# Score and softmax vectors written to HBM from their columns in natural order, without turns on TensorE; second layer's second pass moved into the projection

## The chip, the cores and the metric

The kernel runs on one core of one Trainium2 chip. The metric is device microseconds (us) of one execution. TensorE does the matrix products and writes them to its output memory, PSUM; VectorE and ScalarE work element by element; the sync engine's queue issues transfers between the on-chip memory and HBM, the memory outside the core. A transfer *lands* when it counts as complete, so that what waits for it may go on. The *granted clock* is the mean share of its full clock that TensorE was given in a run. Most executions agree within 0.3%. The kernel before was timed again in each session and took 3140 us in the first and 3148 to 3152 us in the later ones; ratios are always taken within a session.

## The reference, cut to what matters

Two graph attention layers over 32 graphs of 512 nodes, after a normalization and a ReLU; float32 throughout, with the residual x added at the end.

```python
def gat_layer(x, mask, W, a_src, a_dst, bias, concat):
    xl = (x @ W).reshape(B, N, H, F)
    asrc = einsum('bnhf,hf->bnh', xl, a_src)
    adst = einsum('bnhf,hf->bnh', xl, a_dst)
    e = leaky_relu(asrc[:, :, None, :] + adst[:, None, :, :], 0.2)
    e = where(mask[..., None], e, -1e9)
    attn = softmax(e, axis=1)
    out = einsum('bsdh,bshf->bdhf', attn, xl)
    ...
# layer 1: 4 heads of 256 features; layer 2: one head of 512
```

The scores asrc and adst come out of the projection as columns: node t*128+p sits on partition p, column t. The softmax also needs a vector of all 512 nodes laid along the free dimension of every partition. That takes a change of layout, from a column to a row spread over 128 partitions. It happens 8 times a batch: twice for the scores of layer 1 (two heads together), once for those of layer 2, and five times for the softmax result r (four heads and one head). In all there are 96 + 160 = 256 of these spreads.

## The kernel before

The layout change goes through HBM. TensorE turns (transposes) the columns, VectorE copies the turned rows out of PSUM, one transfer writes them as 8 (or 4) rows of 512 bytes, and another reads them back into all partitions. (In this code the names of the tiles are left out, and cuts are marked by dots.)

```python
def spread(self, v, rows, tag, more):
    k = rows * NT
    ps = psum.tile([k, P], F32, tag="tp", bufs=2)
    nc.tensor.transpose(ps, v, identf)              # the turn
    sb = work.tile([k, P], F32, tag="spread")
    nc.vector.tensor_copy(sb, ps)
    dr = dram.tile([k, P], F32, tag=f"d{tag}{k}")
    nc.sync.dma_start(dr, sb)                       # 8 x 512 bytes
    o = work.tile([P, 2, N], F32, tag=f"o{tag}", bufs=2)
    nc.sync.dma_start(o[:, :rows]..., <dr read by all 128 partitions>)
    return o

def first(self, h):     # leaky relu of asr + ad, mask, exp, sums; gives r
    ...                 # reads the spread scores
def second(self, h):    # p = exp(max(rr0 + lo0, rr1) + lo1), masked
    ...                 # reads the spread r
```

TensorE runs in program order; the other engines' instructions are put in order when the kernel is built, by a scheduler that weighs priorities and estimated times. Each engine then works through its list in that order and waits where an input is missing.

## Time and profile before

| | before |
|---|---|
| median of three runs | 3140.7 us (3139.0 to 3141.8) |
| TensorE busy | 3036.8 us, 97% of the profiled span of 3143.5 us |
| VectorE, ScalarE busy | 79%, 57% |
| packets of the DMA engines | 121,530, of which 15,616 under 512 bytes |

The prediction shows the lines that carry its argument. One view that it did not use answers to the main view of the changed kernel: the waits of the sync queue, which issues all transfers. The columns are who waited for what, us in total, times, longest.

```profile
SPq L251 <- DMA drr<-rrr: 120.7, 100, 2.9
SPq L251 <- DMA das<-ras: 61.9, 66, 2.0
```

The queue waits for a turned vector to land before it issues the broadcast that reads it. That is 182.6 us in 166 waits, 1.1 us each; for the other 90 of the 256 it did not have to wait. The profile page of this kernel lists no landing times.

### The profile page before, as it was taken

How to read it: one execution, taken by the hardware profiler on the slowest of the kernel's cores; microseconds unless marked ns; L12 is line 12 of the kernel's file. 1: busy time of each engine (PE TensorE's matmuls, PEld its weight loads, DVE VectorE, ACT ScalarE, POOL GpSimd, SP SyncE). 2: the span in 40 equal slices, each digit the busy share in tenths (PEclk: the TensorE clock that was granted, in tenths of full speed). 3: DMA queues.
4: the chain of work that ended last, by engine and by line, in shares of the span. 5: the costliest groups of instructions: out<-in, count | busy, mean ns of one | idle time of the engine just before them, and what ended most of it. 6: DMA issues, size and time to landing. Idle time of an engine off the chain costs nothing.

```text
span 3143.5 us, 35412 instructions
## 1 busy us (share of the span) xinstructions
PE 3036.8 (97%) x11536; PEld 2027.3 (64%) x11536; DVE 2494.4 (79%) x5663; ACT 1806.2 (57%) x3873; POOL 44.0 (1%) x38
## 2 busy tenths in 40 slices
PE   5899999999999999999999999999999999999997
PEld 4566676676676666676666766666766666766654
DVE  8678887788878888877888877888878788778774
ACT  4556656556656556565566565566565565665651
POOL 0000000000000000000000000000000000000000
PEclk8999999999999999999999999999999999999998
DMA  5122232222232222222222322222322222222211
GB/s 188 44 71 84 84 101 88 81 78 91 85 98 82 86 81 87 88 93 88 71 84 85 101 90 88 74 84 85 101 88 81 78 85 90 96 84 71 65 66 62
DMA packets 121530, 269.38 MB, mean 86 GB/s; under 512 B 15616, under 2 KB 22656, under 8 KB 121344
## 3 DMA queue, kind: packets, MB, share of 16 engines
q1 hardware_dynamic: 121344, 267.12, 25.9%
q8 instruction: 90, 1.47, 0.2%
q14 instruction: 96, 0.79, 0.1%
HBM read 232.53 MB, written 34.54 MB: 85 GB/s over the span
## 4 chain that ended last, share of the span: by engine, by line
PE 78%; DVE 9%; DMA 9%; ACT 1%; SPq 1%; issue 1%; POOL 0%; DVEq 0%; ACTq 0%; POOLq 0%
PE po L414 27%; PE po L477 10%; PE pxm_0a L348 7%; PE pxm_1a L348 7%; DMA orr<-drr 4%; PE pxm_1b L348 3%; PE pxm_0b L348 3%; DVE p L310 3%; PE pxl_2a L348 3%; DVE p L318 3%; PE pxl_3a L348 3%; DMA drr<-rrr 2%; DMA x<-in_x_dram 2%; PE pxl_0a L348 2%; PE pxm_0g L348 2%; PE pxl_3b L348 2%
## 5 line engine op out<-in xcount | busy, mean ns | idle before, releaser
L414 PE MATMUL po<-p,xl 128*128 128x512 f32 x2048 | 894.0, 595 | 9.2 <-DVE p L318 9.2
L414 PEld LDWEIGHTS po<-p,xl 128*128 128x128 f32 x2048 | 388.3, 191 | 484.5 <-issue 452.1
L314 ACT ACTIVATE p<-p,lo 128x512 f32<-128x512 f32 x640 | 442.4, 719 | 254.2 <-DVE p L310 253.1
L284 DVE CUSTOM_DVE_ANT_0 l<-l,mt 128x512 f32<-128x512 f32 x640 | 415.8, 685 | 130.6 <-ACT l L281 129.5
L310 DVE SCALAR_TENSOR_TENSOR p<-orr,lo 128x512 f32<-128x512 f32 x640 | 448.4, 747 | 77.9 <-DMA orr<-drr 77.7
L281 ACT ACTIVATE l<-oas,sc 128x512 f32<-128x512 f32 x640 | 430.4, 711 | 87.8 <-DMA oas<-das 84.2
L288 ACT ACTIVATE l<-l,low 128x512 f32<-128x512 f32 x640 | 455.0, 712 | 37.8 <-DVE low L284 34.7
L477 PE MATMUL po<-xl,p 128*128 128x512 f32 x1024 | 460.6, 594 | 10.0 <-DVE p L318 10.0
L318 DVE TENSOR_TENSOR p<-p,m 128x1024 f32<-128x1024 f32 x320 | 384.2, 1218 | 0.0
L477 PEld LDWEIGHTS po<-xl,p 128*128 128x128 f32 x1024 | 187.8, 191 | 211.4 <-issue 198.8
L420 ACT ACTIVATE e<-po,b_sb 128x512 f32<-128x512 f32 x256 | 172.5, 675 | 160.5 <-PE po L414 159.1
L422 DVE SCALAR_TENSOR_TENSOR h<-po,b_sb,e 128x512 f32<-128x512 f32 x256 | 191.2, 747 | 5.4
L348 PE MATMUL pxm_0a<-w_sb,h 128*128 128x257 f32 x768 | 184.1, 382 | 0.0
L348 PE MATMUL pxm_1a<-w_sb,h 128*128 128x257 f32 x768 | 182.6, 379 | 0.0
L348 PEld LDWEIGHTS pxm_0a<-w_sb,h 128*128 128x128 f32 x768 | 144.0, 191 | 37.7 <-issue 14.0
L421 DVE TENSOR_SCALAR e<-e 128x512 f32<-128x512 f32 x256 | 107.9, 421 | 72.5 <-ACT e L420 68.5
L348 PEld LDWEIGHTS pxm_1a<-w_sb,h 128*128 128x128 f32 x768 | 143.1, 190 | 23.9
L348 PE MATMUL pxm_1b<-w_sb,hs 128*128 128x257 f32 x512 | 123.7, 384 | 5.0 <-DVE hs L331 5.0
L348 PE MATMUL pxm_0b<-w_sb,hs 128*128 128x257 f32 x512 | 121.8, 380 | 0.0
L482 DVE TENSOR_TENSOR xr<-po,xr 128x512 f32<-128x512 f32 x128 | 87.3, 682 | 43.0 <-PE po L477 42.9
L288 ACT ACTIVATION_READ_ACCUMULATOR l<-l,low 128x1 f32 x640 | 120.2, 188 | 0.0
L348 PE MATMUL pxl_0a<-w_sb,ht 128*128 128x258 f32 x372 | 99.2, 389 | 19.5 <-DVE xl L359 19.5
(137 smaller groups left out, 4048.5 us busy)
## 6 DMA issues: line engine op xcount, KB each, us to landing
orr<-drr SPq DMA_DIRECT2D x160, 512.0 KB
x<-in_x_dram SPq DMA_DIRECT2D x128, 256.0 KB
adj<-in_adj_dram SPq DMA_DIRECT2D x128, 256.0 KB
oas<-das SPq DMA_DIRECT2D x64, 512.0 KB
xr<-in_x_dram SPq DMA_DIRECT2D x128, 256.0 KB
out_dram<-xr SPq DMA_DIRECT2D x128, 256.0 KB
oas<-das SPq DMA_DIRECT2D x32, 256.0 KB
drr<-rrr SPq DMA_DIRECT2D x160, 4.0 KB
```

What stands on the lines that cost most here:

```text
L281: nc.scalar.activation(e, self.asr[i][:, j, :], AF.Prelu, bias=ad[:, d : d + 1], alpha=SLOPE)
L284: nc.vector.tensor_tensor_reduce(out=e, in0=e, in1=MASKT[self.b][:, d, :], scale=-1.0, scalar=BIG, op0=OP.add, op1=OP.min, accum_out=low[: ...
L288: nc.scalar.activation(e, e, AF.Exp, bias=low[:, d : d + 1], scale=-1.0, accum_out=tot[:, d : d + 1])
L310: nc.vector.scalar_tensor_tensor(p[:, u, :], rr[:, 0, :], lo[:, 0, j, u : u + 1], rr[:, 1, :], op0=OP.add, op1=OP.max,)
L314: nc.scalar.activation(p[:, u, :], p[:, u, :], AF.Exp, bias=lo[:, 1, j, u : u + 1])
L318: nc.vector.tensor_tensor(pp, pp, MASK[self.b][:, t : t + 2, :], op=OP.min)
L348: nc.tensor.matmul(ps, left[n][:, k, m * P : (m + 1) * P], right(w_sb[:, n - 1], k), start=(first and k == 0), stop=(k == kh - 1), skip_gr ...
L414: nc.tensor.matmul(ps, xl[:, s, h, 2 + f * P : 2 + (f + 1) * P], p[:, s, :], start=(s == 0), stop=(s == NT - 1),)
L420: nc.scalar.activation(e, ps, AF.Exp, bias=bias)
L421: nc.vector.tensor_scalar(e, e, 1.0, -1.0, op0=OP.min, op1=OP.add)
L422: nc.vector.scalar_tensor_tensor(H1[b][:, g, :], ps, bias, e, op0=OP.add, op1=OP.max)
L477: nc.tensor.matmul(ps, p[:, s, d * P : (d + 1) * P], v[:, s, 1 : DO + 1], start=(s == 0), stop=(s == NT - 1),)
```

## The change

The intent is to take the turns off TensorE, which bounds the kernel. The columns are written straight to HBM, each 4-byte element at its natural place. A softmax then no longer asks anything of TensorE, so the passes can be called in another order; the copies that empty PSUM (evacuations) become urgent, and the second pass of layer 2 moves from the start of the projection to its eighth step.

```diff
-            k = rows * NT
-            ps = psum.tile([k, P], F32, tag="tp", name=f"p{tag}{name}", bufs=2)
-            nc.tensor.transpose(ps, v, identf)
-            sb = work.tile([k, P], F32, tag="spread", name=f"r{tag}{name}")
-            nc.vector.tensor_copy(sb, ps)
-            dr = dram.tile([k, P], F32, tag=f"d{tag}{k}", name=f"d{tag}{name}")
-            nc.sync.dma_start(dr, sb)
+            dr = dram.tile([rows, NT, P], F32, tag=f"d{tag}{rows}", name=f"d{tag}{name}", bufs=3)
+            nc.sync.dma_start(dr.rearrange("r t p -> p r t"), v)
...
+            with tc.high_priority(offset=URGENT):      # around each evacuation of PSUM
...
-                        plan[2] = [lambda: late.turn(0), lambda: late.second(0)]
+                        plan[8] = [lambda: step(mt), lambda: late.second(0)]
...
-                        (3, lambda: s1.turn(0)), (3, lambda: s1.first(2)),
-                        (4, lambda: s1.second(0)),
+                        (1, lambda: s1.first(1)), (1, lambda: s1.turn(1)),
+                        (3, lambda: s1.second(0)),
...  (the rest of the new order: each turn is called right behind its first pass)
```

More of the change, by code (lines that the diff above doesn't have):

```diff
@@ L20 @@
 BIG = 2.0**100
+URGENT = 300
 def rows_of(ap, n):
@@ L205, in norm @@
                 nc.tensor.transpose(ps[:, k, :], hn[:, k * P : (k + 1) * P], identf)
-            nc.scalar.activation(HT[b][:, :, t * P : (t + 1) * P], ps, AF.Relu)
+            with tc.high_priority(offset=URGENT):
+                nc.scalar.activation(HT[b][:, :, t * P : (t + 1) * P], ps, AF.Relu)
             yield
@@ L228, in turned_masks @@
                 )
-            nc.vector.tensor_scalar_add(MASKT[b][:, d, :], ps, -BIG)
+            with tc.high_priority(offset=URGENT):
+                nc.vector.tensor_scalar_add(MASKT[b][:, d, :], ps, -BIG)
             yield
@@ L268, in rows @@
             self.asr[i] = self.spread(
-                self.sc[i][:, 0].rearrange("p h t -> p (h t)"), self.g, "as", i
+                self.sc[i][:, 0], self.g, "as", i
             )
@@ L300, in turn @@
         def turn(self, h):
-            self.rr[h] = self.spread(self.r.pop(h).rearrange("p i t -> p (i t)"), 2, "rr", h)
+            self.rr[h] = self.spread(self.r.pop(h), 2, "rr", h)
         def second(self, h):
@@ L351, in sevens @@
                 )
-            if n in (1, 5, 6):
-                nc.scalar.activation(to(*{1: (0, 0), 5: (1, 1), 6: (0, 1)}[n]), ps, AF.Copy)
-            elif n == 4:
-                nc.scalar.activation(to(1, 0), ps, AF.Copy)
-            else:
-                d = to(*{2: (0, 0), 7: (1, 1), 3: (0, 1)}[n])
-                nc.vector.tensor_add(d, ps, d)
+            with tc.high_priority(offset=URGENT):
+                if n in (1, 5, 6):
+                    nc.scalar.activation(to(*{1: (0, 0), 5: (1, 1), 6: (0, 1)}[n]), ps, AF.Copy)
+                elif n == 4:
+                    nc.scalar.activation(to(1, 0), ps, AF.Copy)
+                else:
+                    d = to(*{2: (0, 0), 7: (1, 1), 3: (0, 1)}[n])
+                    nc.vector.tensor_add(d, ps, d)
             yield
@@ L419, in gather1 @@
                 e = work.tile([P, N], F32, tag="xr", name=f"e{b}_{g}", bufs=2)
-                nc.scalar.activation(e, ps, AF.Exp, bias=bias)
-                nc.vector.tensor_scalar(e, e, 1.0, -1.0, op0=OP.min, op1=OP.add)
-                nc.vector.scalar_tensor_tensor(
-                    H1[b][:, g, :], ps, bias, e, op0=OP.add, op1=OP.max
-                )
+                with tc.high_priority(offset=URGENT):
+                    nc.scalar.activation(e, ps, AF.Exp, bias=bias)
+                    nc.vector.tensor_scalar(e, e, 1.0, -1.0, op0=OP.min, op1=OP.add)
+                    nc.vector.scalar_tensor_tensor(
+                        H1[b][:, g, :], ps, bias, e, op0=OP.add, op1=OP.max
+                    )
                 yield
@@ L531, in tile_gat @@
         s1.columns(1)
+        s1.rows(1)
+        s1.first(0)
+        s1.turn(0)
         step(nm)
-        s1.first(0)
-        s1.rows(1)
-        step(nm)
-        s1.turn(0)
         s1.first(1)
+        s1.turn(1)
         s1.second(0)
         step(nm)
-        s1.turn(1)
         s1.first(2)
+        s1.turn(2)
         s1.second(1)
+        step(nm)
+        s1.first(3)
+        s1.turn(3)
+        s1.second(2)
         step(nm)
@@ L561, in tile_gat @@
                     if late:
-                        plan[2] = [lambda: late.turn(0), lambda: late.second(0)]
+                        plan[8] = [lambda: step(mt), lambda: late.second(0)]
                     if i >= 1:
                         plan[14] = [lambda: residual_bias(i - 1)]
-                    plan[20] = [lambda: s1.columns(0)]
-                    plan[24] = [lambda: s1.rows(0), lambda: s1.first(0)]
-                    plan[28] = [lambda: s1.columns(1), lambda: s1.first(1)]
+                    plan[20] = [lambda: s1.columns(0), lambda: s1.rows(0)]
+                    plan[24] = [lambda: s1.first(0), lambda: s1.turn(0)]
+                    plan[28] = [lambda: s1.columns(1), lambda: s1.rows(1)]
                     for n, _ in enumerate(project1(i + 1), 1):
@@ L578, in tile_gat @@
                     for n, f in (
-                        (1, lambda: s1.rows(1)),
-                        (3, lambda: s1.turn(0)), (3, lambda: s1.first(2)),
-                        (4, lambda: s1.second(0)),
-                        (9, lambda: s1.turn(1)), (9, lambda: s1.first(3)),
-                        (10, lambda: s1.second(1)),
-                        (13, lambda: s1.turn(2)),
-                        (14, lambda: s1.second(2)),
-                        (16, lambda: s1.turn(3)),
+                        (1, lambda: s1.first(1)), (1, lambda: s1.turn(1)),
+                        (3, lambda: s1.second(0)),
+                        (4, lambda: s1.first(2)), (4, lambda: s1.turn(2)),
+                        (7, lambda: s1.second(1)),
+                        (9, lambda: s1.first(3)), (9, lambda: s1.turn(3)),
+                        (12, lambda: s1.second(2)),
                     ):
@@ L597, in tile_gat @@
                         15: [lambda: late.rows(0), lambda: late.first(0)],
-                        18: [lambda: late.turn(0), lambda: late.second(0)],
+                        16: [lambda: late.turn(0), lambda: late.second(0)],
                     }
@@ L612, in tile_gat @@
                 if late:
-                    plan[2] = [lambda: late.rows(0), lambda: late.first(0)]
+                    plan[0] = [lambda: late.rows(0)]
+                    plan[2] = [lambda: late.first(0), lambda: late.turn(0)]
                 if i + 2 == B:
-                    plan[6] = [lambda: late.turn(0)]
                     plan[7] = [lambda: late.second(0)]
                 if i < 0:
-                    plan[0] = [lambda: s1.turn(2), lambda: s1.first(3), lambda: s1.second(2)]
-                    plan[2] = [lambda: s1.turn(3), lambda: s1.second(3)]
+                    plan[1] = [lambda: s1.second(3)]
                 else:
```

## The prediction

> **What bounds the kernel now.** I read the page's busy shares first, then TensorE's waits, then its timeline in one steady stretch and at both ends, and last the DMA queue's own rows.
>
> ```profile
> PE 3036.8 (97%) x11536; PEld 2027.3 (64%) x11536; DVE 2494.4 (79%) x5663; ACT 1806.2 (57%) x3873; POOL 44.0 (1%) x38
> PE   5899999999999999999999999999999999999997
> DMA  5122232222232222222222322222322222222211
> ```
>
> TensorE has work in 97% of the span and misses some in the first three slices and the last. So the change can only win what TensorE idles (3143.5 - 3036.8 = 106.7 us), its own removed work, and cold-clock time; 2% is 63 us.
>
> ```profile
> PE prr L245 <- DVE r L295: 40.2, 32, 8.5
> PE pxl_0a L348 <- DVE xl L359: 19.5, 30, 1.5
> PE po L477 <- DVE p L318: 10.0, 1, 10.0
> PE pxm_1b L348 <- DVE hs L331: 5.0, 1, 5.0
> L245 PE MATMUL prr<-identf,r 128*8 128x128 f32 x160 | 43.9, 274 | 40.4 <-DVE r L295 40.2
> L245 PE MATMUL pas<-identf,sc 128*8 128x128 f32 (+1 forms) x96 | 26.1, 272 | 4.1 <-DVE sc L402 4.1
> ```
>
> Columns of the first four: who waited for whom, us in total, times, longest. The largest wait is for the turns the change removes (prr, pas). The second is the first layer's projection waiting for a VectorE addition out of PSUM, once per batch.
>
> ```profile
> 1347.79 1.03 PE L348 MATMUL pxl_0b<-w_sb,hs 128*128 128x258 f32 x4
> 1348.66 0.27 PE L245 MATMUL prr<-identf,r 128*8 128x128 f32 x1
> 1348.77 1.04 PE L348 MATMUL pxl_0g<-w_sb,ht 128*128 128x258 f32 x4
> ...
> 1361.82 1.14 PE L348 MATMUL pxl_0a<-w_sb,ht 128*128 128x258 f32 x4 [0.73 <-DVE xl L359]
> ...
> 1385.07 0.27 PE L245 MATMUL prr<-identf,r 128*8 128x128 f32 x1 [0.42 <-DVE r L295]
> ...
> 148.84 0.37 PE L245 MATMUL prr<-identf,r 128*8 128x128 f32 x1 [8.53 <-DVE r L295]
> 149.01 3.16 PE L348 MATMUL pxm_0a<-w_sb,h 128*128 128x257 f32 x8
> 152.00 1.90 PE L348 MATMUL pxm_1a<-w_sb,h 128*128 128x257 f32 x8
> ```
>
> A turn is 0.27 us long, but the next matmul starts 0.11 us after it, so 0.11 us is its price. After the 8.53 us gap eight matmuls took 3.16 us instead of 1.90.
>
> ```profile
> 26.30 1.58 SPq L149 DMA_DIRECT2D b_sb<-in_L_gnn_b_dram  x1
> 1387.12 0.28 SPq L249 DMA_DIRECT2D drr<-rrr  x1
> 1388.35 0.32 SPq L251 DMA_DIRECT2D orr<-drr  x1
> 1392.29 0.75 DVE L310 SCALAR_TENSOR_TENSOR p<-orr,lo 128x512 f32<-128x512 f32 x1 [1.06 <-DMA orr<-drr]
> 31.50:32.00 0.50, 0.50 (x4) 0.45 (x3) 0.50 (x1) 0.19 (x1) 0.00 (x0) 1.00 1.09 348
> 32.00:32.50 0.50, 0.50 (x4) 0.42 (x4) 0.50 (x3) 0.20 (x1) 0.00 (x0) 1.00 1.24 219
> DMA packets 611, 0.11 MB, mean 219 GB/s; under 512 B 510, under 2 KB 607, under 8 KB 611
> ```
>
> The first row issues the load of the bias in 4-byte elements, 128x8 of them: the same count as a new write of scores. It kept the queue 1.58 us. Today's 4 KB write lands so that the broadcast can issue 1.23 us after it, and the broadcast is usable 3.9 us later. The two windows (last two columns: DMA share and GB/s) price small packets: 31.5 to 32 had 170 packets of about 1 KB in 1.09 x 0.5 x 16 = 8.7 engine-us, 51 ns each; 32 to 32.5 had 611 packets (last row) in 9.9 engine-us, so the 510 small ones took (9.9 - 101 x 0.051) / 510 = 9 ns each.
>
> **What the Trainium skill says.** "DMA: Bandwidth & Descriptors", Rules for kernel authors: a strided last dimension becomes one descriptor per element. The bias load agrees: the small packets are there, and the issue took 1.58 us against 0.28. The same page, Two DMAs through the same engine are not ordered: a DMA that reads what another wrote has to wait for its completion; so write, landing and broadcast stay in series, as L249 and L251 are. "TensorE: Matmul & The Clock Gate", Part 1: after about 3.4 us idle the clock falls to half and needs as long to return; 3.16 against 1.90 us agrees. The same page, Part 4, has a transpose at about 275 ns in one kernel; the rows say 272 to 274, of which 0.11 us is paid in a stream.
>
> **Part by part.** One steady batch of before, from gather to gather (178.67 to 2938.98 us, 29 batches), is 95.2 us. TensorE's timeline splits it: projection one 26.7, second gather 15.0, projection two 26.0, first gather 27.6.
>
> 1. Turns removed: 256 of them, 8 a batch: 8 x 0.11 = 0.9 us a batch on the path. Their PSUM copies leave VectorE (8 x about 0.2 us), beside other work.
> 2. The waits of turns: 40.2 + 4.1 us go wholly, as TensorE no longer stands in the softmax chain; but 22.9 us of it (8.05, 6.27, 8.53) and 2.74 lie in the first 150 us, and 3.43 + 2.55 at the end. Steady share about 0.4 us a batch, with restart about 0.6.
> 3. The 0.65 us wait of pxl_0a: before, VectorE stood at L310 for a broadcast (0.71 us) and then did six second-pass operations (1356.4 to 1361.4) ahead of the addition. In the built order of after, the second layer's pass sits between the additions of the gather before it, and the additions, now urgent, follow each other. Summing VectorE's durations in that order from the last h of the gather (about 3 us into the projection), the addition ends when its matmul does, at about 10.6 us, and is needed at 14. I count 0.6 us gained.
> So the floor is 25.6 + 14.2 + 25.7 + 27.5 = 93.0 us a batch; the rest is rounding.
> 4. The new write, from column to broadcast usable: issue about 1.4, 64 packets per engine x 9 ns = 0.6 beside it, receipt about 1: 2.4 us against 1.23, then 3.9. It saves in turn the wait for TensorE's place, turn and copy: 1.4 to 5.5 us by the rows between r and the write (1384.9 to 1387.1; 1404.95 to 1410.5). The softmax is about 3 us earlier at its start, level at worst later.
> The walk through one batch of after, from projection one's start at 0, takes the built order and net durations (distance to the next start) from the timelines: softmax pass over the mask (L284) 0.61, p (L310) 0.67, p times mask (L318) 1.14, ScalarE's exponentials 0.62 to 0.71. The score columns are ready at 19, and their broadcast at 19 + 0.2 + 2.4 + 3.9 = 25.5 (before: 29.2). VectorE then does sums of h (4 x 1.14), sixteen L284, the store additions and three heads' passes without a rest. Head 0: r at 34, broadcast at 34 + 6.3 = 40, p done at 46. Head 1: r at 39, broadcast at 46, p done at 54. Head 2: r at 51, broadcast at 57, p done at 64. Head 3: r at 59, p done by about 75. The gather takes them at 65.5, 72, 79 and 86. So every head is ready 10 us or more ahead. The tightest points are two additions out of PSUM in projection two: they stand behind head 2's p, end at 59.5 and 61.8, and TensorE wants their banks at 62 and 63.8: about 2 us of slack. I allow 0.3 us a batch for what I miss: 93.3. Steady: 29 x 1.9 = 55 us.
> 5. Start: the first four softmaxes are bound by VectorE (45 of 50 us from 60 to 110), not by turns. But the order of after does less unneeded work ahead of the fourth head, ready about 98.5 instead of 105; that removes the 5.2 us wait in the gather and some of its lag: 7 us. The next batch, without a second gather, takes 66.0 us from projection to gather and needs 52: 12 us after a small allowance.
> 6. End: the last regular batch 1.6 us. In the last gather the turn's wait (3.43), the wait for hs (5.0: the second pass stood before it) and the cold clock after it (2.6) go: 11 us. In the closing chain, score column to first product took 26.1 us (3097.7 to 3123.8), of which TensorE stood 2.55 and 10.04 us; without the turns' places and copies and with slower writes about 23: 3 us.
> Sum: 55 + 19 + 1.6 + 14 = 90 us, 3051. Pieces so computed meet contention I have not seen, so I take off a tenth of the gain or less: 3057.
>
> **Rivals.** *The scattered write is slow.* 1,024 writes of 4 bytes in HBM may be acknowledged more slowly than the reads I priced. For it: no such write is in the trace. Against: the 9 ns and DMA engines busy only a quarter of the time. With 3 us more each, slack of 2 us at the tight additions is gone: 1 us a batch returns, ends lose 6: about 3095. With 8 us more the softmax bounds: slower than before.
> *VectorE takes the bound.* It is busy 75 to 77 of 95 us and nearly gapless in the last 40 us ahead of the gather; waits for broadcasts (77.7 us today) then are not absorbed by turns. Against: it loses work, and the softmax starts earlier. It would leave 1 us a batch: about 3085.
> *Only the urgent order matters:* if the removal of turns merely moves TensorE's idle time to the p tiles, the gain is 0.9 + 0.6 us a batch and little at the ends: about 3090.
> *No losses:* 93.0 a batch and better ends: about 3040.
>
> **Range and chances.** The steady floor, summed from start-to-start distances, is sure to 0.2 us; the losses on top are one-sided. 3036 to 3090 should hold it 8 times in 10. Faster by over 2% (below 3078) has 0.83, within 2% 0.15, slower 0.02.
>
> **What would show it.** Right: TensorE's busy share 99%; no wait for r or sc columns in its list; pxl_0a's wait nearly gone; batches of 93 to 93.5 us; gather one ending near 105 us; new writes issuing in 1.2 to 1.6 us, their broadcasts about 2.4 us after. Wrong: waits of po or pxm for L317 or L359 of a half us or more in each batch; more idle VectorE time before its first p operation on orr than 77.7 us with TensorE waiting behind it; a write-to-broadcast distance over 4 us; or VectorE rows of waits for adj or xr delaying additions.

## The result, and the profile after

The changed kernel took 5084.85 us (median of four runs, 5078.54 to 5091.19) against 3139.86 us before: a ratio of 1.6194 (95% interval 1.6166 to 1.6223). A version that differs from it only in the queue of the broadcasts gave right results. I had given "slower" a chance of 0.02.

The first lines are of its page: busy time, TensorE's and the DMA engines' busy tenths in 40 slices, and the packets.

```profile
PE 3357.5 (66%) x11280; PEld 2216.9 (44%) x11280; DVE 2412.2 (47%) x5407; ACT 1799.1 (35%) x3873; POOL 42.8 (1%) x38
...
PE   4766757667566675666756667666666576675766
...
DMA  4122122221222212222122221222221232212121
...
DMA packets 367542, 269.34 MB, mean 53 GB/s; under 512 B 263552, under 2 KB 268672, under 8 KB 367360
```

No engine is busy more than 66%, and the DMA engines move almost nothing: after the first slice no slice shows more than three tenths. The number of matmuls fell by exactly the 256 turns, and the small packets rose to 263,552. A kernel in which nothing is busy waits in a chain. The chain that ended last, by engine, is the next line (TensorE had 78% of this chain before, DMA 9%):

```profile
DMA 61%; DVE 17%; PE 15%; ACT 2%; issue 2%; SPq 1%; POOL 1%; DVEq 0%; POOLq 0%; ACTq 0%
```

Then TensorE's waits (columns as before). Compare them with the prediction's list, in which the largest was 40.2 us:

```profile
PE pxm_0a L347 <- ACT xl L354: 709.5, 60, 20.6
PE po L414 <- DVE p L317: 365.7, 40, 26.8
PE pxl_1g L347 <- DVE h L423: 352.6, 29, 13.5
```

The first and third are waits for a PSUM bank (one of the pieces of PSUM that TensorE writes in turn). ScalarE and VectorE would need well under 1 us to empty it, 0.37 and 0.75 us, but they stand in their own order behind other operations. What VectorE waited for among the transfers, in the same columns:

```profile
DVE p L309 <- DMA orr<-drr: 895.7, 116, 12.4
DVE stats L193 <- DMA x<-in_x_dram: 692.0, 59, 17.9
```

The first is the second pass of a softmax, which waits for its broadcast; the second is the normalization, which waits for a load of x (8.9 us in all before). What the broadcast waits for is in the waits of the sync queue:

```profile
SPq L250 <- DMA drr<-r: 1501.6, 160, 12.3
...
SPq L250 <- DMA das<-sc: 864.2, 96, 11.9
```

All 256 scattered writes are waited for, 2366 of 5083 us in all, 9.2 us each against 1.1 before. One of them can be followed: first in the queue's timeline (start, duration of the issue), then in the busy tenths of the DMA engines in 40 slices of each of the two microseconds 2218 to 2219 and 2219 to 2220, then in the window after them (window, length, busy PE, PEld, DVE, ACT, POOL, clock, DMA share, GB/s):

```profile
2217.78 0.37 SPq L248 DMA_DIRECT2D das<-sc  x1
2227.01 0.32 SPq L250 DMA_DIRECT2D oas<-das  x1
```

```profile
DMA  0000000000000000000000000001468777777777
DMA  7687677678884100000000000000000000000000
```

```profile
2220.00:2227.00 7.00, 7.00 (x36) 6.08 (x35) 4.64 (x16) 5.77 (x15) 0.00 (x0) 1.00 0.00 0
```

The issue took 0.37 us, not the 1.4 I expected. The engines handled the small packets between about 2218.7 and 2219.4, in some 0.7 us, near the 0.6 that I had priced. Then, for 7.6 us, they moved nothing, and only at 2227 did the write count as landed. So the time lies neither in the issue nor in the moving of the packets, but after it. The page's list of issues (last column: median us from issue to landing) gives the same for all of them:

```profile
drr<-r SPq DMA_DIRECT2D x160, 4.0 KB, 10.3
das<-sc SPq DMA_DIRECT2D x64, 4.0 KB, 9.7
das<-sc SPq DMA_DIRECT2D x32, 2.0 KB, 8.3
```

Half the elements (the last row has 512 of them, not 1,024) save only 1.4 us, so this is not a price per element.

The slow write also holds up what is issued behind it. Here a load of x was issued 0.5 us after a scattered write that landed at 2239.8, and VectorE, idle for 15.8 us, stood for that load until 2240.5:

```profile
2227.89 0.38 SPq L248 DMA_DIRECT2D drr<-r  x1
2228.37 0.66 SPq L178 DMA_DIRECT2D x<-in_x_dram  x1
```

By the landings in the trace, 89 transfers were issued while a scattered write was under way, and none of them landed before it. For loads of x the median to landing was 11.7 us in that case (57 of them) and 4.7 otherwise. The chain that ended last has 35% in scattered writes (drr and das), 12% in broadcasts and 15% in loads of x. So the loss has two paths, the broadcasts and the loads behind them, and both begin with the same landing.

TensorE's clock went down too, from 0.990 to 0.825: the page has 3357.5 us of busy TensorE for 11,280 matmuls, where the version of the second experiment has 2991.0 for as many at 0.990. Of every time below that has long waits of TensorE, a part is this.

### The profile page after: what moved, and what is told of

Its sections match the earlier page's. It is cut to its first block, busy times and chain, and to the rows that moved or that the text cites. A ratio compares the mean times of both kernels' runs of the same rounds, so it can differ in the third digit from the quotient of the medians.

```text
span 5083.1 us, 34627 instructions
## 1 busy us (share of the span) xinstructions
PE 3357.5 (66%) x11280; PEld 2216.9 (44%) x11280; DVE 2412.2 (47%) x5407; ACT 1799.1 (35%) x3873; POOL 42.8 (1%) x38
## 4 chain that ended last, share of the span: by engine, by line
DMA 61%; DVE 17%; PE 15%; ACT 2%; issue 2%; SPq 1%; POOL 1%; DVEq 0%; POOLq 0%; ACTq 0%
DMA drr<-r 19%; DMA das<-sc 16%; DMA x<-in_x_dram 15%; DMA orr<-drr 7%; DVE p L309 6%; DMA oas<-das 5%; DVE l L283 3%; DVE p L317 2%; PE pxl_0a L347 2%; PE pxl_1a L347 2%; PE po L478 1%; DVE h L423 1%; PE pxl_2a L347 1%; PE pxl_3a L347 1%; PE pxl_1g L347 1%
## 5 line engine op out<-in xcount | busy, mean ns | idle before, releaser
L414 PE MATMUL po<-p,xl 128*128 128x512 f32 x2048 | 977.2, 638 | 365.7 <-DVE p L317 365.7
L309 DVE SCALAR_TENSOR_TENSOR p<-orr,lo 128x512 f32<-128x512 f32 x640 | 451.3, 746 | 896.1 <-DMA orr<-drr 895.7
L347 PE MATMUL pxm_0a<-w_sb,hs 128*128 128x257 f32 x256 | 118.3, 641 | 591.9 <-ACT xl L354 585.4
L347 PE MATMUL pxm_0a<-w_sb,h 128*128 128x257 f32 x768 | 281.4, 530 | 335.8 <-DVE xl L359 211.7
L193 DVE BATCH_NORM_STATS2 stats<-x 128x6 f32<-128x512 f32 x128 | 86.4, 676 | 692.0 <-DMA x<-in_x_dram 692.0
L317 DVE TENSOR_TENSOR p<-p,m 128x1024 f32<-128x1024 f32 x320 | 385.8, 1214 | 0.6 <-ACT p L313 0.6
L347 PEld LDWEIGHTS pxm_0a<-w_sb,h 128*128 128x128 f32 x768 | 197.7, 266 | 412.0 <-DVE xl L359 223.8
L347 PEld LDWEIGHTS pxm_0a<-w_sb,hs 128*128 128x128 f32 x256 | 79.4, 325 | 622.4 <-ACT xl L354 602.4
L347 PE MATMUL pxl_1g<-w_sb,ht 128*128 128x258 f32 x124 | 62.8, 660 | 352.6 <-DVE h L423 352.6
L347 PE MATMUL pxm_1a<-w_sb,h 128*128 128x257 f32 x768 | 207.9, 418 | 5.2 <-ACT xl L354 5.2
L347 PEld LDWEIGHTS pxl_1g<-w_sb,ht 128*128 128x128 f32 x124 | 35.5, 315 | 363.1 <-DVE h L423 357.6
L347 PEld LDWEIGHTS pxm_1a<-w_sb,h 128*128 128x128 f32 x768 | 170.6, 222 | 39.7 <-ACT xl L354 5.6
## 6 DMA issues: line engine op xcount, KB each, us to landing
drr<-r SPq DMA_DIRECT2D x160, 4.0 KB, 10.3
```

Source lines behind the costliest of these rows:

```text
L193: nc.vector.bn_stats(stats[:, t, :], XT[b][t])
L309: nc.vector.scalar_tensor_tensor(p[:, u, :], rr[:, 0, :], lo[:, 0, j, u : u + 1], rr[:, 1, :], op0=OP.add, op1=OP.max,)
L317: nc.vector.tensor_tensor(pp, pp, MASK[self.b][:, t : t + 2, :], op=OP.min)
L347: nc.tensor.matmul(ps, left[n][:, k, m * P : (m + 1) * P], right(w_sb[:, n - 1], k), start=(first and k == 0), stop=(k == kh - 1), skip_gr ...
L414: nc.tensor.matmul(ps, xl[:, s, h, 2 + f * P : 2 + (f + 1) * P], p[:, s, :], start=(s == 0), stop=(s == NT - 1),)
```

## The experiments

My theory (A) was that the slow landing of scattered writes is the whole of the loss, and that the rest of the prediction's sum holds. The rivals were that the new order of work or the urgent priorities do the harm, that the blocked sync queue holds back other transfers, or that the turns' absence moves the wait elsewhere.

### Only the write, in the kernel before

```diff
-            nc.tensor.transpose(ps, v, identf) ... nc.sync.dma_start(dr, sb)
+            nc.sync.dma_start(dr.rearrange("r t p -> p r t"), v)
```

> The kernel before, with its own order of work and no urgent priorities, in which only the turn (transpose, PSUM copy, 8x512-byte write) is replaced by the write of single 4-byte elements. Theory A (the landing of that write, 8 to 12 us instead of about 1, lengthens the softmax chain by some 8 us at each of 8 writes a batch): about 3140 + 32 x 64 = 5190 us, 4700 to 5500. Rival B (the new order of work and the urgent priorities did the harm, the write is a small part): within 150 us of 3140.

It took 5177.13 us, ratio 1.6429 (1.6400 to 1.6457). The write alone, in the old order and without priorities, loses even a little more than the whole change. Theory A holds; the rival that the new order did the harm has fallen.

### Everything but the write

The changed kernel keeps its order and its priorities, but VectorE turns the vector in 32x32 blocks, and four transfers write runs of 128 bytes.

```diff
-            nc.sync.dma_start(dr.rearrange("r t p -> p r t"), v)
+            nc.vector.tensor_copy(sq[:, :k], v)          # sq: a [128, 32] pad
+            nc.vector.transpose(tq, sq)                  # 32 x 32 blocks
+            for q in range(P // 32):
+                nc.sync.dma_start(dr...[:, q * 32 : q * 32 + 32], tq[q * 32 : q * 32 + k, :])
```

> The changed kernel, whole plan and priorities kept, but each vector is turned on VectorE (one small copy, one transpose in 32x32 blocks) and written as runs of 128 bytes in four transfers, with no 4-byte elements and no turns on TensorE. Theory A (only the size of the landing was wrong in the prediction, the rest of its steps hold): 3040 to 3090 us. Rival B (the plan or the loss of turns by itself does harm): above 3200. If four transfers of 128-byte runs land as slowly as the 4-byte ones: about 5000.

It took 3059.15 us with right results, ratio 0.9703 (0.9688 to 0.9717): faster than both kernels, and 2 us from the number that I had predicted for the changed kernel. The first line is its busy time, the second TensorE's longest list entry.

```profile
PE 2991.0 (98%) x11280; PEld 2026.0 (66%) x11280; DVE 2492.0 (81%) x5923; ACT 1798.8 (59%) x3873; POOL 34.3 (1%) x38
```

```profile
PE po L428 <- DVE p L331: 23.7, 5, 15.2
```

The waits of turns are gone, and none of the waits in each batch of the changed kernel is left. The prediction's total was therefore reachable, but not with the write that it was made for.

### The priorities alone

> The kernel before with nothing but the urgent priorities around the evacuations of PSUM. Theory A (priorities are a small gain, the wait of 0.65 us at the first layer's projection mostly goes): 3100 to 3135 us. Rival B (urgent evacuations delay the softmax, part of the harm comes from there): above 3150.

The edit is the kernel before with the urgent blocks of the diff and nothing else. It took 3122.72 us, ratio 0.9904 (0.9889 to 0.9919): a gain of 1%, clear of the noise. The rival that the priorities harm has fallen.

### Turns on VectorE in the old order, without and with the priorities

> The kernel before with its own order of work and no priorities; only the turn moves from TensorE to VectorE, written as runs of 128 bytes. If the prediction's first two items hold by themselves (0.9 us a batch of turns and most of the 44 us of waits for turns): 3075 to 3110 us. If the waits only move to the p tiles, as in the rival 'Only the urgent order matters': 3105 to 3130.

It took 3097.28 us, ratio 0.9836 (0.9821 to 0.9851). Taking the turns off TensorE is worth some 52 us by itself (1.64% of 3148).

> The kernel before with its own order of work, turns on VectorE and the urgent priorities. If the two gains add up (ratios 0.9836 and 0.9904 to the kernel before): 0.974, some 3065 us, and the changed order of work is worth less than 0.5%. If the moved second pass and the new order are worth 1% or more: 3090 or more here against 3059 with them.

It took 3063.61 us, ratio 0.9733 (0.9712 to 0.9754), close to the product 0.9836 x 0.9904 = 0.9742. The two gains add up. The new order with its moved second pass, the third part of the change, is left with 0.9733 - 0.9703 = 0.3%; the two intervals overlap, so even that is not clear of the noise.

### The new order with the old turns

> The changed order of work and priorities, but the turns back on TensorE as in the kernel before. The new order puts each turn directly behind its first softmax pass, so TensorE, which works in program order, stands until r is there: some 5 turns a batch by 3 to 6 us, 3140 + 32 x 15 to 32 x 30 = 3600 to 4100 us. If the order of work does not need the turns to be off TensorE: 3060 to 3150.

One run, its state unknown, gave 3997.2 us. TensorE stands for r, as the wait shows:

```profile
PE prr L249 <- DVE r L299: 685.4, 99, 10.8
```

With the old turns the new order loses, so it could not have been tried before the turns were off TensorE.

### The broadcasts on another queue

```diff
-            nc.sync.dma_start(o[:, :rows]...)      # the broadcast only
+            nc.gpsimd.dma_start(o[:, :rows]...)
```

> The changed kernel, with only the broadcast reads issued from GpSimd's queue, so that the wait for a landing no longer holds up the loads of x, adj and the stores on the sync queue. Theory A (the chain column, scattered write, landing, broadcast, softmax is what bounds: latency): 4700 to 5100 us. Rival (the sync queue, blocked 2366 of 5083 us, holds back other transfers, and that is most of the loss): 3300 to 4200.

One run, its state unknown, gave 5218.79 us, 119 above the upper end of theory A and 1000 above what the rival allows. With the landing waited for elsewhere, the sync queue was free to issue the other transfers, and nothing was gained: that the loads are issued late is not the loss. But the run does not free the loads. Issued behind a scattered write they still landed after it (148 of 148 such transfers), loads of x took 12.2 us to land in the median, and VectorE waited longer for them than in the changed kernel (busy us, mean ns of one, idle before and what ended it):

```profile
L193 DVE BATCH_NORM_STATS2 stats<-x 128x6 f32<-128x512 f32 x128 | 88.2, 691 | 730.0 <-DMA x<-in_x_dram 730.0
```

How the loss divides between late broadcasts and late loads, no run separates.

### Only the three score vectors scattered

```diff
+            if tag == "as":  (4-byte elements, as in the changed kernel)
+            else:            (VectorE's turn, as in the second experiment)
```

> The kernel with VectorE's turns and the changed plan (3059 us), in which only the score vectors (3 of the 8 a batch) are written as single 4-byte elements. If each scattered write lies on the softmax chain with its full extra of some 8 us: 3059 + 32 x 3 x 8 = 3830, 3600 to 3900. If a softmax that starts later is hidden behind the projections as the prediction counted (10 us ahead at the gather): 3060 to 3300.

It took 3839.77 us, ratio 1.2182 (1.2161 to 1.2202). The extra over the version with all vectors turned is 3839.8 - 3059.2 = 780.6 us; by 32 batches and 3 writes that is 8.1 us for each scattered write. From the start of a write of scores to its broadcast the median is 9.8 us here and 2.3 us with all vectors turned (means 9.8 and 3.3), so the extra is 6.5 to 7.6 us. Each write costs at least that, and nothing of it was hidden behind the projections. What goes beyond it has TensorE's clock in it (0.913 against 0.990, 179 us more of busy TensorE) and VectorE's waits for loads of x (271 us against 22).

### The writes by themselves

A kernel without the GAT (wrong result) sends one transfer at a time, waits, reads 512 bytes back and goes on. In the first try the transfers were not held in program order:

> No GAT at all (wrong result on purpose): one transfer at a time on one queue, each waited for and 512 bytes of it read back before the next; six of each kind. Expected landing of the write. Theory 1 (writes that fall into the same 64 bytes are done one after the other, sixteen of them at some 0.5 us each): the natural order lands in 8 to 10 us with eight, four, two and one column alike; elements 64 or 512 bytes apart land in 2 to 3 us; pairs of 8 bytes about half, 4 to 5 us; eight elements of one partition side by side are as slow if only the shared line matters. Theory 2 (each 4-byte write costs, whatever stands beside it): the landing falls with the count, about 9, 5.5, 3.7 and 2.8 us for eight, four, two and one column, and elements far apart are as slow as neighbours, 9 us. Both: rows of 32, 128 and 512 bytes land in 1.5 to 3 us. Reads of 1,024 single elements: 2 to 3 us under theory 1, 8 under theory 2.

The scheduler laid the kinds of writes over each other, so their landings could not be told apart; it showed nothing that I use. In the second try the queue keeps its order:

> The kinds of writes of the first try again, now held in strict program order on the queue, so that the start of each 512-byte read behind a write marks the landing of that write. Theory 1 (writes into the same 64 bytes wait for each other): eight, four, two and one column in natural order land alike, 8 to 10 us; elements 64 or 512 bytes apart in 2 to 3 us; pairs in 4 to 5 us. Theory 2 (each 4-byte write costs something of its own, whatever stands beside it): about 9, 5.5, 3.7 and 2.8 us for eight, four, two and one column; elements far apart as slow as neighbours, 9 us. In both, rows of 32, 128 and 512 bytes land in 1.5 to 3 us, and 1,024 reads of 4 bytes in about 2 us (the first try had 2.3).

These are waits of the sync queue for the write to land, after its issue of about 0.4 us (who waited for what, us in total, times, longest; "eight" and "one" are 1,024 and 128 elements in natural order, "gapline" is 1,024 elements each 64 bytes apart, "rowshort" is 128 rows of 32 bytes side by side):

```profile
SPq L88 <- DMA dnateight<-src: 39.3, 4, 10.9
...
SPq L88 <- DMA dnatone<-src: 27.8, 4, 7.3
...
SPq L88 <- DMA dgapline<-src: 8.9, 4, 2.3
...
SPq L88 <- DMA drowshort<-src: 4.3, 4, 1.1
```

From the start of the write to the start of the read behind it, the means of four are:

| kind of write | writes | to landing, us |
|---|---|---|
| natural order, 8 / 4 / 2 / 1 columns | 1024 / 512 / 256 / 128 | 10.3 / 9.2 / 8.3 / 7.3 |
| the same 1,024 elements, 16 / 64 / 512 bytes apart | 1024 | 3.3 / 2.7 / 2.6 |
| 8 elements of one partition, 8 bytes apart | 1024 | 6.2 |
| pairs of 8 bytes, natural order | 512 | 3.8 |
| rows of 32 / 128 / 512 bytes | 128 / 32 / 8 | 1.5 / 1.4 / 1.3 |

Theory 2, a price for each 4-byte write, has fallen twice over. An eighth of the writes still takes 7.3 us where it had 2.8, and the same 1,024 writes land in 2.7 us once they stand apart. In this kernel the spaced elements go into a piece of HBM that was overwritten as a whole just before, and the dense ones into one that only the repetition before had written; the full kernel below, which zeroes the piece only once, at the start, gives about the same 2.7 us, so this was not the reason. Theory 1 holds in kind: what costs is how close together in HBM the written pieces stand. Its number for one column was 8 to 10 and 7.3 came out, so the count adds a little. Reads are not concerned: 1,024 reads of 4 bytes took about 2.5 us from one to the next, a small copy between them included.

A third kernel varied the step:

> One transfer at a time again. 1,024 elements of 4 bytes at steps of 4, 8, 16, 32 and 64 bytes. If what counts is how many writes share 64 bytes, each waiting some 0.5 us: 10, 6.2, 3.4, 2.9, 2.7 us from the write's start to the landing; if the shared piece is 32 bytes, 32 and 64 are equal, and if it is larger than 64 bytes nothing levels off before 64. One column (128 elements): 7.3 close together, about 2 at 64 bytes. Runs of 16 bytes (256 writes) about 3, runs of 32 bytes 1.5 us.

For steps of 4, 8, 16, 32 and 64 bytes, the means of five were 10.5, 4.5, 3.2, 2.9 and 2.7 us. The 8-byte step was nearer to the pairs than to my 6.2. Most of the price is gone at 16 bytes, and it does not level off sharply at a size of piece that I could name. One column, close together and 64 bytes apart:

```profile
SPq L88 <- DMA dcolumn<-src: 36.0, 5, 7.5
...
SPq L88 <- DMA dcolumnfar<-src: 5.3, 5, 1.1
```

The same 128 writes waited 7.2 us each, or 1.1. Runs of 16 bytes landed in 2.2 us in the mean (1.6 to 3.0), runs of 32 bytes in 1.5.

### The same writes, 64 bytes apart, in the full kernel

```diff
-            dr = dram.tile([rows, NT, P], ...)
-            nc.sync.dma_start(dr.rearrange("r t p -> p r t"), v)
+            dr = <one of three tiles [rows, NT, P, 16], zeroed at the start>
+            nc.sync.dma_start(dr[:, :, :, 0].rearrange("r t p -> p r t"), v)
```

> The changed kernel with the same 1,024 writes of 4 bytes, the same issues and the same broadcasts, but in HBM the elements stand 64 bytes apart, so that no two share 64 bytes. The broadcast still reads 4 KB in one piece, so it spreads wrong numbers (wrong result on purpose; the time does not depend on them). Theory (the loss is only that writes close together in HBM wait for each other; alone, such a write landed in 2.7 us, near the 2.4 us of the prediction): 3045 to 3100 us. Rival (many 4-byte writes are slow in the full kernel however they stand): above 4000.

It took 3217.26 us, ratio 1.0217 (1.0188 to 1.0246). Its output is wrong, which doesn't matter for the time. With the same number of 4-byte writes, 5084.9 - 3217.3 = 1868 us of the loss is gone, so the rival that such writes are slow in the full kernel however they stand has fallen. But my range ended at 3100. One wait that comes in each batch was left, and the landing was 2.9 us for r:

```profile
PE pxl_1g L359 <- DVE h L435: 97.6, 29, 5.0
```

```profile
drr<-r SPq DMA_DIRECT2D x160, 4.0 KB, 2.9
```

VectorE's timeline of one batch shows why (the bracket is idle time and what ended it): behind the sixth evacuation of the gather, it stood for layer 2's broadcast, did four operations of the second pass, and came to the seventh evacuation, the one that frees the bank, after 2270.

```profile
2265.88 2.74 DVE L321 SCALAR_TENSOR_TENSOR p<-orr,lo 128x512 f32<-128x512 f32 x4 [3.97 <-DMA orr<-drr]
...
2270.01 0.75 DVE L435 SCALAR_TENSOR_TENSOR h<-po,b_sb,e 128x512 f32<-128x512 f32 x1
```

Two more runs asked whether this order or the landing is to blame.

> The changed kernel's own order and operations, but each partition writes its 16 or 32 bytes in one piece (128 rows side by side; alone such a write landed in 1.45 us). The numbers arrive in the wrong order on purpose. If only the order costs and the landing is free slack: about 3217 still. If each us of landing is paid in each batch at the late bank: 3.4 - 1.25 = 2.15 us of wait left, about 3217 - 29 x 1.25 = 3180, or some 20 lower with a warmer clock. If the landing is the whole cause: 3060.

Each partition writes its numbers in one piece (in the wrong order):

```diff
-            nc.sync.dma_start(dr.rearrange("r t p -> p r t"), v)
+            nc.sync.dma_start(dr.rearrange("r t p -> (r t p)").rearrange("(p r t) -> p r t", r=rows, t=NT), v)
```

It took 3045.28 us, ratio 0.9671 (0.9655 to 0.9687), with a landing of 1.4 us:

```profile
drr<-r SPq DMA_DIRECT2D x160, 4.0 KB, 1.4
```

In the traces VectorE's and ScalarE's sequences are the same, instruction for instruction, as in the changed kernel, and the 64-byte version differs from them only in the first 294 of VectorE's 5,408 instructions and the first 95 of ScalarE's 3,873. The three kernels thus do the same work in the same order, but for the start, with three landings. The mean landing weighted by the 8 writes of a batch (five r, two and one of scores) is 9.9, 2.7 and 1.4 us:

| landing, us | time, us | step, us | 256 x the landing saved, us |
|---|---|---|---|
| 9.9 (the changed kernel) | 5085 | | |
| 2.7 (64 bytes apart) | 3217 | 1868 | 256 x 7.2 = 1843 |
| 1.4 (rows in one piece) | 3045 | 172 | 256 x 1.3 = 333 |

The step from 9.9 to 2.7 us is as large as if each microsecond of landing were paid in full at each of the 256 spreads; the one from 2.7 to 1.4 is about half of that. The sums are a measure, not a mechanism: the steps also contain the loads held up behind the writes (VectorE waited 692, 82 and 42 us for x) and TensorE's clock (0.825, 0.979 and 0.993, with 3357.5, 3042.4 and 2989.2 us of busy TensorE for the same matmuls).

> Elements 64 bytes apart as before (landing 2.7 us; wrong result on purpose), but written from a copy turned on VectorE, so that the built order of VectorE has the evacuation of h that frees the awaited bank ahead of the second layer's second pass. If the order is the cause of the remaining 158 us: 3050 to 3090 us. If the landing of 2.7 us is the cause: 3190 or more.

```diff
+            nc.vector.tensor_copy(sq[:, :k], v)
+            nc.vector.transpose(tq, sq)
-            nc.sync.dma_start(dr[:, :, :, 0].rearrange("r t p -> p r t"), v)
+            nc.sync.dma_start(dr[:, :, :, 0].rearrange("r t p -> p r t"), tq[:, :k]...)
```

It took 3286.04 us, ratio 1.0435 (1.0419 to 1.0450). The evacuation did come first, but TensorE's wait moved to another bank, which ScalarE frees (92.8 us in 29 waits), so putting that one evacuation first is no cure. This run is not clean: the two added operations led the scheduler to shift many others, so it cannot say what the order is worth. It stays open whether some order would hide a landing of 2.7 us. The version with VectorE's turns, at 3059 us, suggests one. From its first write to its broadcast it leaves 3.5 us in the median for the r of layer 1 (2.9 with the elements 64 bytes apart), and for the r of layer 2, behind which the awaited bank stood, 2.3 us (against 2.8), read from the queue's timelines. In the stretch of its timeline that I read, the seventh evacuation (1588.99) comes ahead of layer 2's second pass (1591.76), and TensorE does not wait there.

### The quick rows, read right

```diff
+            nc.sync.dma_start(dr, v)                     # dr: [P, k], a row in one piece
+            nc.sync.dma_start(o[:, : rows * N], <dr read by all partitions>)
+            return o[:, : rows * N].rearrange("p (q r t) -> p r t q", r=rows, t=NT)
```

> The changed kernel, with each partition writing its 8 (or 4) numbers in one piece, the broadcast copied as it stands, and ScalarE and VectorE reading it in steps of 32 (16) bytes, so that the result is right. If reading by steps costs nothing (the score activation stays near 710 ns and the second pass's first operation near 746 ns): 3035 to 3060 us, faster than the changed order with VectorE's turns (3059). If a stepped read takes twice the time, both engines gain some 20 x 0.7 us a batch: 3300 or more.

It took 3486.42 us with right results, ratio 1.1070 (1.1051 to 1.1088). The rows landed in 1.4 us, but the readers paid. First this kernel's two groups that read the broadcast by steps, then the same in the kernel with the wrong order of numbers (busy us, mean ns of one, idle before):

```profile
L280 ACT ACTIVATE l<-oas,sc 128x512 f32<-128x512 f32 x640 | 766.8, 1227 | 366.3 <-DMA oas<-das 330.6 <-DVE xl L360 26.7 <-DVE j L160 7.9
L309 DVE SCALAR_TENSOR_TENSOR p<-orr,lo 128x512 f32<-128x512 f32 x640 | 705.3, 1143 | 83.3 <-DMA orr<-drr 74.7 <-PE pxl_0g L348 5.0 <-PE pxl_1a L348 3.4
```

```profile
L311 DVE SCALAR_TENSOR_TENSOR p<-orr,lo 128x512 f32<-128x512 f32 x640 | 451.5, 746 | 84.3 <-DMA orr<-drr 82.9 <-PE po L416 0.7
L282 ACT ACTIVATE l<-oas,sc 128x512 f32<-128x512 f32 x640 | 437.6, 712 | 263.5 <-DMA oas<-das 245.6 <-DVE xl L361 13.3 <-DVE j L160 3.5
```

ScalarE's operation went from 712 to 1227 ns and VectorE's from 746 to 1143. The hope of beating 3059 us this way has fallen; the second reading of the expectation, 3300 or more, came true. The Trainium skill, "SBUF — State Buffer", Door 1: The DMA port swizzle (its note on SBUF cachelines), says that accesses are at full rate only while at least two fall into the same 16 bytes; these steps are 16 and 32 bytes, and the durations agree.

## Why the prediction was wrong

**The step that failed first is part 4's landing**, the time from the start of the new write to its broadcast: "issue about 1.4, 64 packets per engine x 9 ns = 0.6 beside it, receipt about 1: 2.4 us". In the write followed above, the issue took 0.37 us, the packets were done 1.6 us after the issue began (0.7 us of moving, near the 0.6), and then came 7.6 us until the write counted as landed: the term "receipt about 1" is the one that was mis-sized. I took the issue from a load of 4-byte elements and the packets' price from the same load; a load does not show what a write waits for at its end, and "about 1" for that had no row behind it. The kernel before could not show it, since it has no write of that kind and its page gives no landings. The Trainium skill, "DMA: Bandwidth & Descriptors", Anatomy of one DMA — SWDGE (gpsimd) path, says of transfers issued by GpSimd (these are issued by the sync engine) that completion, not setup, is most of a transfer's fixed cost, and that waiting for the write "can cause a surprisingly long delay especially when the write target is HBM." The trace agrees in kind (idle engines from 2219.4 to 2227), in far larger size than the page's 2 us, and the experiments add what makes it long: writes that stand close together. The prediction did not draw on this section. Nor did it foresee that transfers issued behind such a write land only after it.

**The second failure is the slack.** The prediction had every head "ready 10 us or more ahead" and "about 2 us of slack" at the tightest additions. The landings of 2.7 against 1.4 us in the same order cost 172 us, so not even these 1.3 us were free in that order; the order built for VectorE's turns had no such wait at 2.3 to 3.5 us. The walk followed the gather's readiness for each head and the additions of the projections. It left out the bank that the fifth group of the first projection takes over from the gather (the wait of pxl_1g for h), behind layer 2's second pass. The rival of "3 us more each" (3095) erred by the same missing place: 64-byte steps added only some 0.3 us to the 2.4 I assumed, and took 3217.

**What held.** Parts 1 and 2, the turns and their waits, are real: 52 us with turns on VectorE. The priorities of part 3 alone give 30 us (0.96% of 3152), and the prediction's 0.65 us wait goes with them. The kernel with VectorE's turns shows how the rest of the sum fares, in the prediction's own three stretches (us, first matmul of a gather to first matmul of a gather, by the traces):

| stretch | before | turns on VectorE, new order | gain | predicted gain |
|---|---|---|---|---|
| start, to the second gather | 178.5 | 164.3 | 14.2 | 19 |
| the 29 batches | 2760.3 | 2698.5 | 61.8 | 55 |
| from there to the end | 204.6 | 195.7 | 8.9 | 15.6 |

A batch takes 93.05 us, and 93.3 were predicted. That the total of 3057 met 3059 within 2 us is in part luck: the batches won 7 us more and the two ends 11 less than predicted. And the start's gain does not come from the new order, as part 5 has it: the old order with turns on VectorE and priorities has 163.0 us there, and is worse only at the end, with 200.6. One sum of the prediction does not follow from its rows: the smaller of the two distances behind "1.4 to 5.5 us" is 2.2 us (1384.9 to 1387.1). That changes nothing in its total. And the DMA shares behind its 51 and 9 ns, 1.09 and 1.24, are over 1, so packets overlap in them; by the same measure the 1,040 packets of the two microseconds followed above took 7 ns each (22.1% and 24.6% of 16 engines).

The scattered-write rival named the right outcome, "With 8 us more the softmax bounds: slower than before", and even the right number. What failed was its weight: against it stood the busy share of the DMA engines and a price per packet, neither of which bears on a landing.

**The signs I had set** worked. Of those for "wrong", three came: a write-to-broadcast distance over 4 us (9.2 us in the write followed above), waits of po and pxm for L317 and L359 of more than a half us a batch (365.7 and 211.7 us in all), and more idle VectorE time before its operations on orr than 77.7 us (895.7).

## What to carry to other kernels

Price a write to HBM by its landing, not by its issue or its packets, and measure that landing alone before a chain is built on it; elements of 4 bytes side by side took 7 to 10 us here, rows of 32 bytes or more 1.5. Here the engines work in a fixed order, and a longer landing was paid by all of them: quick evacuations stood behind the operation that waited, and loads issued behind the write landed after it. Turning a small vector on an engine with time to spare (VectorE's 32x32 blocks, two operations of about 0.2 us) kept the whole gain that the change was after, and a layout that only moves the turn into the readers' steps did not.

## What the Trainium skill lacked or had wrong

- "DMA: Bandwidth & Descriptors" has small descriptors as slow to move and a fixed cost of about 2 us; it has nothing on the landing of small writes that stand close together in HBM. Here 128 writes of 4 bytes side by side landed in 7.3 us, and 64 bytes apart in 1.4; 1,024 of them in 10.3 and 2.7, the engines idle for most of it.
- The same page gives 512 bytes as the least for full rate, with read-modify-write below it. In these runs rows of 32 bytes landed as fast as rows of 512 to within 0.2 us (1.5 against 1.3), so for a landing the size was no threshold there.
- "VectorE: DVE Perf Modes", The three transpose paths, calls a turn by a plain strided copy slow when the innermost step at the destination is large (19 times slower than the DMA's own transpose, which no run here used). Here the larger step landed sooner: 1,024 elements with an innermost step of 512 bytes (natural order, eight columns) took 10.3 us, and with one of 8,192 bytes (64 bytes from node to node) 2.7. The nearness of the pieces decided, not that step.
- "SBUF — State Buffer" gives the rule for steps in bytes but no price for ScalarE or VectorE. Here steps of 16 and 32 bytes in float32 took 1227 against 712 ns on ScalarE and 1143 against 746 on VectorE.
